# Loading Delta * u for a selective scan in two rounds of six channels, with five state buffers and loads four units ahead

## The chip, the cores and the metric

One Trainium2 chip; the kernel runs on one of its cores. The metric is the device time of one execution in microseconds (us), lower is better. Before the change three runs took 12,270.65, 12,278.37 and 12,295.46 us; their median, 12,278.37 us, is the time before. A core has five engines with a queue each: PE (matrix products), DVE (vector), ACT (activation functions), POOL (a second, slower vector engine) and SP, which here only issues DMAs; sixteen DMA engines move the data between the memory outside (DRAM) and the on-chip memory of 128 partitions.

## The reference, cut to what matters

The program is a small image network of four layers on an input of 4 x 64 x 64 x 96. Layers 0 and 1 are the costly ones. Each normalises the image, expands 96 to 192 channels, convolves 3 x 3, and runs a selective scan over the 4,096 pixels in four directions (rows, columns, and both backwards). Layers 2 and 3 are attention without softmax and a small feed-forward net. The scan, for each image, direction k, channel e and state n (16 states):

```python
# u: the convolved input, d = softplus(...): Delta, b and c: 16 numbers a step each
def step(h, inp):
    u, d, b, c = inp
    dA = jnp.exp(d[..., None] * A)
    h = dA * h + d[..., None] * b[:, :, None, :] * u[..., None]
    y = jnp.einsum('bken,bkn->bke', h, c)
    return (h, y)
```

So each step of each state needs Delta (for the decay), Delta * u (the same for all 16 states of a channel), b and c, and leaves h, which is summed over the states with c into y.

## The kernel before

The images are taken in two pairs, and each of layers 0 and 1 is run for each pair: four phases (`Scans.run`, L701). A phase has a preparation (`prepare`, L151), beside which the last phase's `finish` runs, and then a scan phase (`scan_phase`, L471). Preparation leaves in DRAM, for each chunk of 512 pixels: Delta, split in three bfloat16 parts (`ph.delta`), two copies of Delta * u (`ph.du`), and b and c (`ph.bc`). The token layers (L723 on) come last.

The 128 partitions of a scan hold 4 groups of states x 8 (direction, image) pairs x 4 states; a row of partitions is a state's number. The scan phase goes through 8 chunks of 512 pixels, and in each through 16 blocks of EB = 12 channels: 128 units, in that order. A unit is a tile h of 128 x 12 x 512 float32, which is 3 MB. Its life:

- `load` (L386): SP issues one DMA for Delta's parts (`load_delta`, L374, tile dlt, 72 partitions, L379) and six for Delta * u (`load_quarters`, L396, L401), which is replicated over the states on the way: partitions 32 to 95 take both DRAM copies, the upper quarter (96 to 127) the second copy, the lower quarter (0 to 31) the first. Each of the three is loaded in two halves of six channels. The middle two quarters are one DMA of 768 KB per half, a quarter is one of 384 KB.
- `times_b` (L408): POOL multiplies three channels at a time by b, in place, four times a unit, half a unit ahead of the scan. The first and second need the first six channels of all partitions, the third and fourth the other six.
- `replicate` (L413) and `decay` (L419): PE spreads Delta to the 128 partitions, ACT takes the exponential, channel by channel, four and three channels ahead.
- `scan` (L425): DVE runs the recurrence over 512 pixels, one instruction a channel, and overwrites Delta * u with h.
- `contract` and `evict` (L437, L454): while the next unit is scanned, PE sums h with c into y and ACT copies y out, in four parts. `store` (L462) then writes y to DRAM in four DMAs of 48 KB on SP.

The scan phase is written in a fixed order (`manual_schedule`): each engine takes its instructions in the order in which the loop (L508 to L539) names them. At the end of unit `at` SP stores unit `at - 1` (L533), loads b or c of a later chunk where one is due (L535, L537), and loads unit `at + 3` (L539). `h` has four buffers and dlt three, so unit `at + 3` takes the buffer of h that unit `at - 1` has just left. Before the loop, the prologue (L493 to L507) loads b of chunk 0, unit 0, c of chunk 0, units 1 and 2, and c of chunk 1. ACT makes the contraction's weights out of c (`weights`, L357): for chunk 0 in the prologue, for the next chunk two at a time during the units from the third on (L527).

A DMA's completion is counted on one of eight semaphores in turn, so in the program each DMA of SP in the scan phase also waits for the DMA that was issued eight before it.

Of the kernel before, what the change touches and what calls it, by code (L numbers as in the profile page):

```python
# [9 lines left out]
F32 = mybir.dt.float32  # L10
F16 = mybir.dt.float16
BF16 = mybir.dt.bfloat16
# [17 lines left out]
TC = 512  # L30
NC = L // TC
ROWS = TC // HW
EB = 12
# [4 lines left out]
DROWS = 3 * NP16 * G  # L38
DC = EB // 3
# [43 lines left out]
class Consts:  # L83
# [3 lines left out]
    def load(self, pool, name, shape):  # L87
        t = pool.tile(shape, F32, name=name)
        self.nc.sync.dma_start(t, self.a[name])
        return t  # L90
# [40 lines left out]
class Scans:  # L131
# [19 lines left out]
    def prepare(self, ph):  # L151
# [16 lines left out]
        with self.tc.tile_pool(name="prep", bufs=1) as wp, self.tc.tile_pool(  # L168
# [3 lines left out]
            def load(name, shape, at=0):  # L172
                t = wp.tile([at + shape[0]] + shape[1:], F32, name=name)
                nc.sync.dma_start(t[at:], a[pre + name])
                return t

            xp = load("x_proj", [C, 2, 2, XD2])
            dt_w = load("dt_w", [XD2 - 2 * NS, 2, E], at=2 * NS)
            conv_b = load("conv_b", [C, 2])
            ds = load("Ds", [C, 2, K])  # L180
            dsum = wp.tile([C, 2], F32, name="dsum")
# [192 lines left out]
    def load_delta(self, u):  # L374

        nc, ph = self.nc, u.ph
        u.dl = self.units.tile([DROWS, DC, TC], BF16, name="dlt", bufs=3)
        at = u.eb * EB
        nc.sync.dma_start(  # L379
            u.dl.rearrange("p e t -> p (e t)"),  # L380
            ph.delta[u.c][:, :, at : at + EB].rearrange(
                "n g (h e) t -> (n g) h (e t)", h=EB // DC
            ),
        )

    def load(self, u):  # L386

        nc, ph = self.nc, u.ph
        u.h = self.units.tile([128, EB, TC], F32, name="h", bufs=4)
        self.load_delta(u)  # L390
        n = EB // 2
        for first, quarters in ((1, 2), (3, 1), (0, 1)):
            for e in range(0, EB, n):
                self.load_quarters(u, e, n, first, quarters)

    def load_quarters(self, u, e, n, first, quarters):  # L396
# [74 lines left out]
    def scan_phase(self, ph):  # L471

        nc = self.nc
        units = [self.Unit(ph, c, eb) for c in range(NC) for eb in range(NEB)]
        last = len(units)

        def ahead(t, do):
            at, n = divmod(t, EB)  # L480
            if at < last:
                do(units[at], n)

        def b_at(t):
            at, n = divmod(t + B_LEAD, EB)
            if n % ER == 0 and 0 <= at < last:
                self.times_b(units[at], n // ER)

        with self.tc.tile_pool(name="units", bufs=2) as self.units, self.tc.tile_pool(
            name="p_a", bufs=6, space=PSUM  # L490
        ) as self.p_a, self.tc.tile_pool(name="p_y", bufs=2, space=PSUM) as self.p_y:
            with self.tc.manual_schedule():
                self.start_phase(ph)  # L493
                self.load_b(ph, 0)
                self.load(units[0])
                self.load_c(ph, 0)
                self.load(units[1])
                self.load(units[2])
                self.load_c(ph, 1)
                for t in range(-B_LEAD, 0, ER):  # L500
                    b_at(t)
                for op in range(16):
                    self.weights(ph, 0, op)
                for t in range(LEAD):
                    ahead(t, self.replicate)
                for t in range(LEAD - 1):
                    ahead(t, self.decay)  # L507
                for at, u in enumerate(units):  # L508
                    before = units[at - 1] if at else None
                    for n in range(EB):  # L510
                        t = at * EB + n
                        ahead(t + LEAD, self.replicate)
                        ahead(t + LEAD - 1, self.decay)
                        self.scan(u, n)
                        q, part = divmod(n, 3)
                        if before:
                            if part < 2:
                                self.contract(before, q, part)
                            else:
                                self.evict(before, q)  # L520
                            if n == 4 and before.c < NC - 1:
                                e = before.eb * EB
                                nc.scalar.copy(
                                    ph.carry[:, e : e + EB], before.h[:, :, TC - 1]
                                )
                        b_at(t)
                        if n == 1 and u.eb >= 2 and u.c + 1 < NC:  # L527
                            self.weights(ph, u.c + 1, u.eb - 2)
                        if n == 7 and u.eb >= NEB - 2 and u.c + 1 < NC:
                            self.weights(ph, u.c + 1, u.eb)  # L530
                        if n == EB - 1:
                            if before:
                                self.store(before)  # L533
                            if u.eb == 8 and u.c + 1 < NC:
                                self.load_b(ph, u.c + 1)  # L535
                            if u.eb == NEB - 1 and u.c + 2 < NC:
                                self.load_c(ph, u.c + 2)  # L537
                            if at + 3 < last:
                                self.load(units[at + 3])  # L539
                for q in range(4):  # L540
                    self.contract(units[-1], q, 0)
                    self.contract(units[-1], q, 1)
                    self.evict(units[-1], q)
                self.store(units[-1])
# [446 lines left out]
```

## Time and profile before

| | |
|---|---|
| median of three runs | 12,278.37 us |
| the profiled execution | 12,285.39 us, span 12,283.6 us |
| first to last scan, four phases | 1,875.7, 1,871.6, 1,874.3 and 1,874.0 us |
| busy, of the span | PE 76%, DVE 76%, ACT 58%, POOL 60% |
| SP's queue of DMAs | 2,163 MB, 52.6% of sixteen engines' time |
| h from du, in all | 1,024 DMAs of 768 KB and 2,048 of 384 KB |

The span is the time from the program's first instruction to its last in one profiled execution. Busy shares are means over stages with different limits: preparation, scan and token layers follow one another, so no engine can be judged by its share of the whole. A group's row names line, engine, operation and tiles (out<-in), the shape and count, then the busy time and the mean duration of one in ns, then the idle time of that engine just ahead of the group and what ended most of it. A wait's row names who waited for whom, the total in us, how often, and the longest. Instructions of SP only issue; the DMA goes on after them.

### The profile page before, as it was taken

To read this page: it belongs to the slowest core of one execution; us is meant where nothing else is said; L and a number is where in the kernel's file an instruction comes from. 1 tells how busy PE (TensorE), PEld (TensorE's weight loads), DVE (VectorE), ACT (ScalarE), POOL (GpSimd) and SP (SyncE) were. 2 spreads that over 40 slices of the span, in tenths; PEclk is the share of its full clock that TensorE was granted. 3 is DMA by queue.
4 is the path that set the end of the run, shared out by engine and by line. 5 is a ranking of instruction groups with operands and counts; after the bars stand their busy time and mean duration, and the time that the engine had idled before them with its cause. 6 is when DMAs were issued, how large, how long until landed. Compare 5 with 4: busy or idle time off the path is not lost.

```text
span 12283.6 us, 340681 instructions
## 1 busy us (share of the span) xinstructions
PE 9393.5 (76%) x147008; PEld 4897.8 (40%) x147008; DVE 9369.7 (76%) x9235; ACT 7066.9 (58%) x11815; POOL 7389.7 (60%) x2316
## 2 busy tenths in 40 slices
PE   7757777769877777769877777778877777777777
PEld 2224444433334444433334444443334444444333
DVE  2479999963569999982569999993459999993667
ACT  2456666643456666653456666662446666662556
POOL 0159999950149999970129999980119999990000
PEclk8669898889778988889778988888778888988787
DMA  3577777754667777764667777764567777773110
GB/s 94 170 226 256 251 252 252 251 166 140 205 206 253 251 252 255 252 201 123 183 206 253 252 251 254 251 226 125 173 194 250 253 253 252 252 252 124 19 21 11
DMA packets 906195, 2491.48 MB, mean 203 GB/s; under 512 B 278030, under 2 KB 560756, under 8 KB 773236
## 3 DMA queue, kind: packets, MB, share of 16 engines
q1 hardware_dynamic: 578036, 2163.43, 52.6%
q10 hardware_dynamic: 326656, 306.25, 8.5%
q8 instruction: 1158, 18.97, 0.7%
q14 instruction: 345, 2.83, 0.1%
HBM read 1955.47 MB, written 513.80 MB: 201 GB/s over the span
## 4 chain that ended last, share of the span: by engine, by line
DMA 57%; PE 20%; SPq 9%; DVE 5%; ACT 4%; issue 3%; POOL 1%; ACTq 1%; DVEq 0%; POOLq 0%
DMA h<-du 51%; SPq L401 8%; PE c L263 8%; PE f L596 2%; PE d L309 2%; DMA yk<-y 2%; DMA delta<-parts 1%; PE c L292 1%; PE f L687 1%; PE f L605 1%; DMA du<-du_sb 1%; POOL parts L323 1%; PE f L676 1%; DVE parts L324 1%; PE f L662 1%
## 5 line engine op out<-in xcount | busy, mean ns | idle before, releaser
L411 POOL TENSOR_TENSOR h<-h,b 128x1536 f32<-128x1536 f32 x2048 | 7019.3, 3461 | 603.8 <-DMA h<-du 230.7
L428 DVE TENSOR_TENSOR_SCAN h<-a,carry,h 128x512 f32<-128x512 f32 x5376 | 6346.6, 1259 | 238.3 <-POOL h L411 231.9
L421 ACT ACTIVATE a<-a,a_col 128x512 f32<-128x512 f32 x6144 | 4030.4, 664 | 1917.7 <-PE a L417 1885.8
L446 PEld LDWEIGHTS y<-h,cw 128*32 128x32 f32 x131072 | 2789.8, 129 | 3520.4 <-issue 1302.1
L446 PE MATMUL y<-h,cw 128*32 128x48 f32 x131072 | 3663.3, 266 | 537.8 <-DVE h L428 210.6
L417 PE MATMUL a<-dlt,rep 72*128 72x512 bf16 x6144 | 2562.4, 428 | 1339.9 <-DVE h L428 1242.8
L323 POOL CAST parts<-dl 96x1024 bf16<-96x1024 f32 x256 | 342.1, 1351 | 3108.6 <-DVE dl L320 2742.6
L319 DVE TENSOR_TENSOR du_sb<-dl,xc 96x1024 f32<-96x1024 f32 x256 | 397.0, 1577 | 1294.6 <-ACT dl L317 1242.0
L458 ACT COPY d<-y 128x384 f32<-128x384 f32 x2048 | 979.7, 478 | 490.5 <-PE y L446 449.4
L263 PE MATMUL c<-xn,taps 96*96 96x512 f32 x2304 | 1036.8, 611 | 73.7 <-DVE xn L248 52.8
L428 DVE TENSOR_TENSOR_SCAN h<-a,h 128x512 f32<-128x512 f32 x768 | 873.0, 1203 | 176.9 <-ACT a L421 139.2
L417 PEld LDWEIGHTS <-rep 72*128 72x128 bf16 x6144 | 490.8, 99 | 888.7 <-issue 646.5
L309 PE MATMUL d<-xd,dt_w 7*96 7x512 f32 x1024 | 523.0, 859 | 260.0 <-ACT xd L295 227.4
L263 PEld LDWEIGHTS c<-xn,taps 96*96 96x96 f32 x2304 | 383.6, 168 | 709.9 <-issue 631.2
L828 POOL MEMSET tn<- 1x4096 f32 x8 | 28.0, 3533 | 863.2 <-PE pa L848 514.2
L270 ACT ACTIVATE xc<-c,conv_b 96x512 f32<-96x512 f32 x128 | 87.3, 682 | 716.0 <-PE c L263 646.4
L596 PE MATMUL f<-yk,perm 128*128 128x384 f32 x1024 | 417.3, 547 | 96.6 <-DMA yk<-y 87.2
L324 DVE TENSOR_TENSOR parts<-dl,parts 96x1024 bf16<-96x1024 f32 x256 | 366.9, 1455 | 154.3 <-POOL parts L323 154.3
L317 ACT ACTIVATE dl<-d 96x1024 f32<-96x1024 f32 x256 | 252.0, 1017 | 402.3 <-DMA delta<-parts 230.6
L292 PE MATMUL c<-xc,x_proj 96*103 96x512 f32 x512 | 422.1, 961 | 2.5 <-ACT xc L270 2.5
L309 PEld LDWEIGHTS d<-xd,dt_w 7*96 7x96 f32 x1024 | 152.3, 212 | 548.3 <-ACT xd L295 299.0
L363 ACT ACTIVATE cw<-c,gmask 128x256 f32<-128x256 f32 x512 | 285.7, 569 | 119.2 <-DMA c<-bc 61.9
(114 smaller groups left out, 5656.7 us busy)
## 6 DMA issues: line engine op xcount, KB each, us to landing
h<-du SPq DMA_DIRECT2D x1024, 768.0 KB
h<-du SPq DMA_DIRECT2D x2048, 384.0 KB
delta<-parts ACTq DMA_DIRECT2D x512, 288.0 KB
dlt<-delta SPq DMA_DIRECT2D x512, 288.0 KB
du<-du_sb SPq DMA_DIRECT2D x256, 384.0 KB
du<-du_sb ACTq DMA_DIRECT2D x256, 384.0 KB
y<-d SPq DMA_DIRECT2D x2048, 48.0 KB
yk<-y SPq DMA_DIRECT2D x256, 384.0 KB
```

Of the source, the lines that this page charges most:

```text
L263: nc.tensor.matmul(rows(ps[:C]), taps[:, tap, h * C : (h + 1) * C], xn[:, ROWS * c + dy : ROWS * (c + 1) + dy, dx : dx + HW], start=tap == ...
L292: nc.tensor.matmul(rows(ps[:XD2]), xp[:, k, h], u[:, h], start=h == 0, stop=h == 1)
L309: nc.tensor.matmul(ps[:, m], dt_w[part, k, m * C : (m + 1) * C], xd[part], start=True, stop=True)
L324: nc.vector.tensor_tensor(parts[:, 2], delta, parts[:, 1], ALU.subtract)
L401: self.nc.sync.dma_start(u.h[32 * first : 32 * (first + quarters), e : e + n].rearrange("p e t -> p (e t)"), source.rearrange("a g e t -> ...
L411: self.nc.gpsimd.tensor_tensor(h, h, b, ALU.mult)
L417: self.nc.tensor.matmul(u.a[n], self.cst.rep[:, h], u.dl[:, e], start=True, stop=True)
L421: self.nc.scalar.activation(u.a[n], u.a[n], AF.Exp, scale=u.ph.a_col[:, at : at + 1])
L428: self.nc.vector.tensor_tensor_scan(u.h[:, n], u.a.pop(n), u.h[:, n], 0.0 if u.c == 0 else u.ph.carry[:, at : at + 1], ALU.mult, ALU.add,)
L446: self.nc.tensor.matmul(view(u.y[32 * j : 32 * j + 32], l2 * EB, (8 * EB, 4), (1, EB)), u.ph.cw[u.c][:, l1, 8 * j + l2], view(u.h, 64 * l1 ...
L458: self.nc.scalar.copy(u.d[:, :, :, l1], u.y[:, : 32 * EB].rearrange("p (t h x) -> p t h x", t=4, h=2))
L596: nc.tensor.matmul(ps[:, : 4 * C].rearrange("p (w v e) -> p w v e", w=4, v=nv), cst.perm[:, k], view(t, off, (sw if k < 2 else -sw, 4), (1 ...
```

## The change

The six loads of a unit come in two rounds of six channels; in a round the middle quarters come first, then the lower, then the upper quarter. There are five buffers of h and four of dlt. The prologue loads unit 3 as well, ahead of c of chunk 1, and the loop loads unit `at + 4`, into the buffer that unit `at - 1` has left. What is loaded, how large each DMA is, and all work of the other engines stay as they were.

```diff
     def load_delta(self, u):
-        u.dl = self.units.tile([DROWS, DC, TC], BF16, name="dlt", bufs=3)
+        u.dl = self.units.tile([DROWS, DC, TC], BF16, name="dlt", bufs=4)
...
     def load(self, u):
-        u.h = self.units.tile([128, EB, TC], F32, name="h", bufs=4)
+        u.h = self.units.tile([128, EB, TC], F32, name="h", bufs=5)
         self.load_delta(u)
         n = EB // 2
-        for first, quarters in ((1, 2), (3, 1), (0, 1)):
-            for e in range(0, EB, n):
+        for e in range(0, EB, n):
+            for first, quarters in ((1, 2), (0, 1), (3, 1)):
                 self.load_quarters(u, e, n, first, quarters)
...
                 self.load(units[1])
                 self.load(units[2])
+                self.load(units[3])
                 self.load_c(ph, 1)
...
-                            if at + 3 < last:
-                                self.load(units[at + 3])
+                            if at + 4 < last:
+                                self.load(units[at + 4])
```

## The prediction

> **What bounds the kernel now.** I read the page's chain first, then its groups, the waits of the SP queue, the chain of one stretch, and the busy time of short stretches. From the page, what the DMAs moved in 40 slices, and the shares of the chain by engine and by line:
>
> ```profile
> GB/s 94 170 226 256 251 252 252 251 166 140 205 206 253 251 252 255 252 201 123 183 206 253 252 251 254 251 226 125 173 194 250 253 253 252 252 252 124 19 21 11
> ...
> DMA 57%; PE 20%; SPq 9%; DVE 5%; ACT 4%; issue 3%; POOL 1%; ACTq 1%; DVEq 0%; POOLq 0%
> DMA h<-du 51%; SPq L401 8%; PE c L263 8%; PE f L596 2%; PE d L309 2%; DMA yk<-y 2%; DMA delta<-parts 1%; PE c L292 1%; PE f L687 1%; PE f L605 1%; DMA du<-du_sb 1%; POOL parts L323 1%; PE f L676 1%; DVE parts L324 1%; PE f L662 1%
> ```
>
> Half of the chain is `DMA h<-du`, the loads of Delta * u in the four scan phases (each about 1,874 us, from the first to the last scan), where the rate is flat at 250 to 256 GB/s. But POOL and DVE look nearly full too, by the groups:
>
> ```profile
> L411 POOL TENSOR_TENSOR h<-h,b 128x1536 f32<-128x1536 f32 x2048 | 7019.3, 3461 | 603.8 <-DMA h<-du 230.7
> L428 DVE TENSOR_TENSOR_SCAN h<-a,carry,h 128x512 f32<-128x512 f32 x5376 | 6346.6, 1259 | 238.3 <-POOL h L411 231.9
> ```
>
> Scans start 1.175 us apart when nothing is late (the median in the trace), so a unit of twelve needs 14.10 us of DVE; four POOL products need 4 x 3.46 = 13.84. Between 1100 and 2500 us there are 1144 scans, so a unit takes 1400 / (1144 / 12) = 14.69. DVE waits for POOL, POOL for h. Who holds h up? The SP queue's waits over the run (total us, times, longest):
>
> ```profile
> SPq L401 <- DMA h<-du: 2362.9, 1448, 3.9
> ...
> SPq L379 <- DMA h<-du: 627.0, 493, 3.6
> ...
> SPq L466 <- DMA h<-du: 344.4, 448, 3.2
> ```
>
> and the chain from 1820 to 1845 us (start, us, what):
>
> ```profile
> 1826.45 12.09 DMA h<-du
> 1838.54 0.02 issue
> 1838.56 0.69 SPq L401
> ```
>
> A load is issued 0.02 us after an earlier one has landed; SP hardly waits for a free buffer: in the program's instruction list every SP DMA waits for the DMA issued eight before it. With eleven DMAs a unit, SP is less than one unit ahead in the transfers, whatever the buffers allow. The last question is whether the DMA engines are full. Columns: stretch, busy time of five engines, clock, DMA share of 16, GB/s.
>
> ```profile
> 1844.20:1846.00 1.80, 1.80 (x50) 1.01 (x43) 1.80 (x2) 1.22 (x4) 1.80 (x1) 0.82 0.59 231
> 1835.60:1838.50 2.90, 2.73 (x67) 1.58 (x67) 2.90 (x4) 1.75 (x5) 2.85 (x2) 1.00 1.01 302
> 752.50:755.50 3.00, 0.00 (x0) 0.00 (x0) 0.00 (x0) 0.00 (x0) 0.00 (x0) 0.50 1.02 218
> 1100.00:2500.00 1400.00, 1079.69 (x25506) 609.54 (x25497) 1348.06 (x1144) 956.34 (x1705) 1302.79 (x381) 0.89 0.74 252
> ```
>
> Call the loads M (partitions 32 to 95), U (96 to 127) and L (0 to 31), each for channels 0 to 5 (0) and 6 to 11 (1); a dash marks the next unit. The completions say which is running: row one is U0 alone, 9 of 16 engines; row two L with M' beside it, all 16, 302 GB/s; row three, in the first unit of a phase, U0 with M' beside it: all 16 busy, yet only 218 GB/s. In the packet records at least eight transfers run 99% of the time from 1200 to 2100 us. So eight engines never rest, the other eight are half idle, and a unit lasts as long as those eight need.
>
> [...] M has 16 source rows and runs on all 16[...]. The trace agrees: 141 completion packets a unit, where 2 x 16 (M), 4 x 8 (quarters), 12 (dlt) and 4 x 16 (y) make 140. [...] a 12 KB packet takes 0.464 us alone, 0.92 to 0.95 with U beside M', about 0.6 with L beside M'. (That the source copy, which U shares with upper M', collides instead would have the same effect.)
>
> **The change, part by part.** *Present cost of a unit*, from mean gaps between successive completions, 1100 to 2500 us: dlt 1.04, M0 1.69, M1 1.95, U0 1.90, U1 1.88, L0 2.64, L1 2.48, four y 1.07: 14.65, as above. A half-block of four packets alone is 4 x 0.464 = 1.86; L0 and L1 together carry 1.40 more, because dlt' and M' run beside them. Everything else: 13.25.
>
> *The new order* M0 L0 U0 M1 L1 U1 has the same DMAs and bytes; what moves is who waits for what, eight back. Now: dlt' for U0, M0' for U1, M1' for L0, so M' runs beside L. After: dlt' for U0, M0' for M1, L0' for L1, U0' for U1, M1' for the first y. From the completion that frees it, a load needs 0.05 to start, 0.65 to issue (L401's median) and 0.6 to 1.15 (at 742 to 745 us) until packets flow: about 1.6. So:
> - M0' flows 1.6 us after M1 has landed. L1 takes 1.86, or about 2.35 with dlt' beside it as L0 has now (+0.5). One upper packet of M0' fits there; three meet U1 at double time: U1 + 3 x 0.464 = +1.4.
> - M1' is issued some 0.7 after U1, flows 2.3 after, beside dlt' and M0' (lower half[...]) and the start of L0': 0.545 a packet as in the 16-wide stretches without a collision, 4 x 0.08 = +0.3 on M0, +0.1 on L0. It ends 4.5 us after U1; U0' begins at 1.07 + 1.04 + 2.0 + 1.95 = 6.1.
> - Sum 13.25 + 0.5 + 1.4 + 0.3 + 0.1 = 15.55, or +0.9 a unit.
>
> The bounds: U1's collision is 2.5 to 4 packets (1.16 to 1.86), dlt's part 0.4 to 0.8, M0 and L0 0.15 to 0.7: +0.3 to +1.95 a unit. A b or c load between y and dlt (13 of 128 units) shifts the waits by one: M0' then waits for L1 and meets only U1's end, so these gain about 0.4. The first five units of a phase collide already (U0 3.84, U1 2.03 in unit 1); I take 0 there, between -10 and +10. Per phase 110 x 0.9 - 13 x 0.4 = 94 us, four phases +375.
>
> *Fifth h, fourth dlt buffer, loads four ahead.* No instruction more; each load stands one unit earlier in SP's program. With SP held by loads eight back it doesn't start earlier, so 0. Should transfers become the faster side, it would be worth part of DVE's 276 us below. *POOL may start* after the third load, not the fifth; that shifts the unit, not its period. Its second pair then waits for U1, 7.5 us after U0, against 6.9 of work.
>
> *The prologue.* Unit 3's seven DMAs pass the c load of chunk 1, which lands about 15 us later (798.95 now). ACT needs it for `weights` early in unit 2 (about 801); behind that in ACT's queue wait decays and evictions, and DVE for them. Up to 14 us a phase, but the loads of units 4 and 5 are already free to run and DVE catches up 1.4 a unit: 0 while transfers bound, +56 in all otherwise.
>
> Against the profiled execution (12,285.4 us, span 12,283.6): 12,660; the median of the runs is 7 lower: 12,653, rounded to **12,650**.
>
> **Rivals.** *Deep prefetch wins (faster).* If the collision misses U1 because M0' starts later or L1 finishes later, transfers fall below 14.1 and DVE bounds. DVE's idle time before scans is 238.3 + 176.9 (the carry-less group) less 139.2 at the four starts = 276 us: 12,002. The point that decides: upper M0' must lose less than 1.4 - 0.9 = 0.5 us to U1, one packet. For it: SP's multiple waits at M0. Against: M0' issue now follows its releasing completion within 0.1 us. *Neutral:* the eight engines carry 24 packets of h in either order, and if collisions only move, the unit stays 14.65: 12,280. Against: 218 against 302 GB/s. *Heavy:* M1' also meets U0'; the starting units, where both do, take 17.1 to 17.9; +2.5 x 440 = 13,380. Against: the 1.6 us of room before U0'.
>
> **How the numbers follow.** Forecast 0.83, faster 0.08, neutral 0.05, heavy 0.04. The forecast's bounds are +0.3 x 440 - 21 (the b and c units) = +111 and +1.95 x 440 - 21 = +837: 12,390 to 13,115. Leaving out the three rivals (0.17) and the last 0.03 at the top, where every bound would have to be at its worst, gives 12,380 to 13,000. About 0.2% is what a measurement can tell from no change: slower 0.88 (forecast, heavy and a little of neutral), same 0.04, faster 0.08.
>
> **What would show it.** Between 1100 and 2500 us some 90 units, not 95; GB/s near 238; DVE and POOL with more idle time, released by h; gaps of 3.3 us before U1's completion and about 2 before U0's; DMA share up though the rate falls. If U1 takes 1.9, the collision is wrong; if DVE's scans stand 1.175 apart throughout, prefetch was the bound.

## The result

The changed kernel takes 13,043 us (median of four runs, 13,031 to 13,052) where the kernel before takes 12,277: a ratio of 1.062, interval 1.060 to 1.064. The forecast was 12,650 with a range to 13,000: right in direction, half of the loss. The profiled span is 13,045.2 us. The four scan phases take 2,061, 2,059, 2,084 and 2,064 us against 1,874 on average, in sum 772 us more. So the loss is wholly in the scan phases, at 1.5 us a unit on average over 512 units.

The page after the change, what the DMAs moved in 40 slices and the shares of the chain:

```profile
GB/s 96 174 222 227 228 228 229 229 173 133 206 205 230 227 230 228 227 206 122 180 208 225 227 226 226 225 225 119 167 202 229 225 228 228 228 228 157 36 20 10
...
DMA 61%; PE 18%; SPq 8%; DVE 4%; ACT 4%; issue 3%; POOL 1%; ACTq 1%; DVEq 0%; POOLq 0%
DMA h<-du 55%; SPq L401 8%; PE c L263 8%; PE f L597 2%; PE d L309 2%; DMA yk<-y 1%; DMA delta<-parts 1%; PE c L292 1%; POOL parts L323 1%; PE f L606 1%; PE f L688 1%; PE f L677 1%; DVE parts L324 1%; DMA du<-du_sb 1%; DVE dl L320 1%
```

The plateau of the scan phases falls from 250 to 256 GB/s to 222 to 230, and the loads hold 55% of the chain, not 51%. The last columns of the groups are the idle time ahead of them, in us:

```profile
L411 POOL TENSOR_TENSOR h<-h,b 128x1536 f32<-128x1536 f32 x2048 | 7028.5, 3454 | 1367.2 <-DMA h<-du 621.6
L428 DVE TENSOR_TENSOR_SCAN h<-a,carry,h 128x512 f32<-128x512 f32 x5376 | 6405.8, 1261 | 889.9 <-POOL h L411 870.4
```

POOL and DVE do the same work in the same time (3.454 and 1.261 us each; an elementwise product or sum of POOL's shape, 128 x 1536 in float32, takes DVE 1.74 to 1.76 us, L650, L651 and L670) and wait 763 and 652 us longer, POOL mostly for h, DVE for POOL. PE's granted clock is lower after the change, 0.806 of full speed against 0.845, but PE holds 18% of the chain, not 20%, so this doesn't bound. SP's waits for loads (total, times, longest) grow from 3,334 to 4,220 us in the three rows:

```profile
SPq L401 <- DMA h<-du: 2639.6, 1477, 3.8
...
SPq L466 <- DMA h<-du: 811.0, 562, 3.6
...
SPq L379 <- DMA h<-du: 769.5, 496, 3.5
```

The chain from 1,500 to 1,530 us (start, us, what; L401 issues a load) has the same look as before the change, and its period can be read off it:

```profile
1512.65 0.02 issue
1512.67 0.68 SPq L401
...
1514.73 14.11 DMA h<-du
1528.84 0.02 issue
1528.86 0.68 SPq L401
```

From one release of SP to the next, 1512.65 to 1528.84, is one unit: 16.19 us. SP issues within 0.02 us of U1's completion, then sits behind the next one. Short stretches of the kernel after (columns as in the prediction):

```profile
1100.00:2500.00 1400.00, 1015.95 (x23083) 563.02 (x23082) 1232.61 (x1035) 823.07 (x1549) 1183.35 (x345) 0.84 0.74 228
1516.20:1518.80 2.60, 0.71 (x17) 0.30 (x10) 2.48 (x3) 2.60 (x7) 2.60 (x2) 1.00 0.90 249
1519.20:1522.60 3.40, 2.60 (x68) 1.51 (x67) 3.40 (x4) 2.83 (x5) 2.05 (x2) 1.00 0.55 222
```

The first row gives 1,035 scans in 1,400 us, 86 units. The other two show the eight engines that carry the quarters with company and without. Where these engines stand can be read from the semaphore counts in the trace. From 1100 to 2500 us each load M has 16 counts and each quarter nine: one 1.1 us after its issue (median) and eight from 4.0 us on, which I read as the ends on its engines. The first y store behind a unit's last quarter has 16 counts, of which eight came ahead of that quarter's first end and eight behind its ends, one by one, in all 86 units (before the change in all 95). I read this as one group of eight that carries the quarters, each engine ending its DMAs in the order of issue, and another eight that run ahead. The records don't say which half of M those other eight carry. I take it to be the upper one, because U beside them pays the double price: of the 50 packets of 12 KB that start from 752.5 to 755.5 us before the change, 43 last over 0.90 us.

After U1's completion at 1512.65, seven of the eight engines of L0 end it at 1513.15 to 1514.19 and U0 at 1517.55 to 1518.82; the last one ends M0 at 1516.15 and L0 at 1518.99. So at 1516 seven engines run U0 and only one runs L0, with the upper half of M1 beside them: 0.90 of the engines busy, 249 GB/s. At 1519 the eight with the quarters run almost alone: 0.55 busy, 222 GB/s. The other eight engines add 27 GB/s.

Here is where the time went, in mean us between successive completions, 1100 to 2500 us. A completion is the end of the last engine of a load; what the other engines did meanwhile comes further down. The last column is the fastest kernel below.

| load | before | forecast | after | e12 |
|---|---|---|---|---|
| dlt | 1.04 | 1.04 | 0.74 | 0.74 |
| M0 | 1.69 | 1.99 | 1.77 | 2.20 |
| M1 | 1.95 | 1.95 | 1.85 | 2.50 |
| L0 | 2.64 | 1.96 | **2.94** | 1.69 |
| L1 | 2.48 | 2.36 | **2.68** | 1.90 |
| U0 | 1.90 | 1.90 | 2.09 | 1.92 |
| U1 | 1.88 | 3.28 | **3.08** | 2.28 |
| y stores | 1.07 | 1.07 | 1.04 | 1.20 |
| sum | 14.65 | 15.55 | 16.19 | 14.43 |

### The profile page after: what moved, and what is told of

Read it like the earlier page. It is cut to its first block, busy times and chain, and to the rows that moved or that the text cites. A ratio compares the mean times of both kernels' runs of the same rounds, so it can differ in the third digit from the quotient of the medians.

```text
span 13045.2 us, 340148 instructions
## 1 busy us (share of the span) xinstructions
PE 9622.6 (74%) x147008; PEld 4963.4 (38%) x147008; DVE 9422.8 (72%) x9235; ACT 6818.8 (52%) x11815; POOL 7399.6 (57%) x2316
## 3 DMA queue, kind: packets, MB, share of 16 engines
q8 instruction: 1158, 18.97, 0.6%
q14 instruction: 341, 2.79, 0.1%
## 4 chain that ended last, share of the span: by engine, by line
DMA 61%; PE 18%; SPq 8%; DVE 4%; ACT 4%; issue 3%; POOL 1%; ACTq 1%; DVEq 0%; POOLq 0%
DMA h<-du 55%; SPq L401 8%; PE c L263 8%; PE f L597 2%; PE d L309 2%; DMA yk<-y 1%; DMA delta<-parts 1%; PE c L292 1%; POOL parts L323 1%; PE f L606 1%; PE f L688 1%; PE f L677 1%; DVE parts L324 1%; DMA du<-du_sb 1%; DVE dl L320 1%
## 5 line engine op out<-in xcount | busy, mean ns | idle before, releaser
L428 DVE TENSOR_TENSOR_SCAN h<-a,carry,h 128x512 f32<-128x512 f32 x5376 | 6405.8, 1261 | 889.9 <-POOL h L411 870.4
L421 ACT ACTIVATE a<-a,a_col 128x512 f32<-128x512 f32 x6144 | 3975.4, 680 | 1047.9 <-PE a L417 1029.4
L446 PEld LDWEIGHTS y<-h,cw 128*32 128x32 f32 x131072 | 2819.7, 132 | 3904.9 <-issue 2557.3
L417 PE MATMUL a<-dlt,rep 72*128 72x512 bf16 x6144 | 2753.0, 453 | 1822.5 <-DVE h L428 1743.1
L458 ACT COPY d<-y 128x384 f32<-128x384 f32 x2048 | 1024.5, 500 | 2209.9 <-DMA y<-d 1551.5
L417 PEld LDWEIGHTS <-rep 72*128 72x128 bf16 x6144 | 528.1, 100 | 1206.9 <-issue 904.1
```

The lines of the kernel that those rows point to most:

```text
L417: self.nc.tensor.matmul(u.a[n], self.cst.rep[:, h], u.dl[:, e], start=True, stop=True)
L421: self.nc.scalar.activation(u.a[n], u.a[n], AF.Exp, scale=u.ph.a_col[:, at : at + 1])
L428: self.nc.vector.tensor_tensor_scan(u.h[:, n], u.a.pop(n), u.h[:, n], 0.0 if u.c == 0 else u.ph.carry[:, at : at + 1], ALU.mult, ALU.add,)
L446: self.nc.tensor.matmul(view(u.y[32 * j : 32 * j + 32], l2 * EB, (8 * EB, 4), (1, EB)), u.ph.cw[u.c][:, l1, 8 * j + l2], view(u.h, 64 * l1 ...
L458: self.nc.scalar.copy(u.d[:, :, :, l1], u.y[:, : 32 * EB].rearrange("p (t h x) -> p t h x", t=4, h=2))
```

## The experiments

Times are medians of four runs (twenty for e2b, buffers and lead alone, and for the first of the three with twelve DMAs); each ratio is to the kernel before on the same chip, with its interval. M, U, L, 0, 1 and the dash are the names of the prediction; "gaps" are those of the table above.

### Which part of the change

**Order alone.** The new order in the kernel before, with four buffers and three units ahead.

```diff
-        for first, quarters in ((1, 2), (3, 1), (0, 1)):
-            for e in range(0, EB, n):
+        for e in range(0, EB, n):
+            for first, quarters in ((1, 2), (0, 1), (3, 1)):
```

> The kernel before with the new order of the six loads alone (M0 L0 U0 M1 L1 U1), four buffers of h, three of dlt, loads three units ahead. If the order is the whole cause: as after, 13,040 us within 40, a unit 16.0 to 16.1 us. If the fifth buffer, the unit more of lead or the later load of c is the cause: 12,280 within 60. A time between divides the loss between the two.

13,053 us, 1.0617 (1.0590 to 1.0643): the order is the whole loss.

**Buffers and lead alone.** Five h, four dlt, loads four units ahead, the old order.

> Five buffers of h, four of dlt and loads four units ahead, with the order of the loads as before. If the order is the whole cause and SP is held by the load eight back: 12,280 within 40, a unit 14.65. If lead and buffers are worth something where transfers are not slowed: down to 12,100. If they are the cause of the loss: about 13,040.

12,303 us, 1.0013 (1.0006 to 1.0020). With SP held by the load eight back, a fifth buffer brings nothing that can be measured. The small loss fits the prediction's late c load at a phase's start: there the slowest unit of a phase, the third, takes 24.5 to 25.8 us, where it took 13.4.

### Which neighbour is slow

**Source copies exchanged** (the changed kernel; the upper quarter reads copy 0, the lower copy 1).

```diff
-        copies = slice(0, 2) if quarters == 2 else slice(first % 2, first % 2 + 1)
+        copies = slice(0, 2) if quarters == 2 else slice(1 - first % 2, 2 - first % 2)
```

> The kernel after with the source copies of the two quarters exchanged: U (partitions 96 to 127) reads copy 0, L (0 to 31) copy 1; the upper half of M still reads copy 1. Two theories of why U1 beside the next M0 is slow. Write side (the partitions of U and of upper M): nothing changes, 13,040 within 40, the gap before U1's completion stays near 3.1 us and that before L0's near 2.9. Source side (both read copy 1): U1's gap falls to about 2.4 and L0's and L1's rise, to 3.7 and 3.2, since they then share the copy; the time may change little, the gaps tell.

13,057 us, 1.0622 (1.0606 to 1.0637). U1 3.01, L0 2.71, L1 2.81: the time doesn't follow the copy.

**Lower quarter first** (the kernel before, whose M' runs beside the last two quarters; these are now U0 and U1).

```diff
-        for first, quarters in ((1, 2), (3, 1), (0, 1)):
+        for first, quarters in ((1, 2), (0, 1), (3, 1)):
```

> The kernel before with the two quarters exchanged in the order, all else as before: M0 M1 L0 L1 U0 U1, so that the next unit's M, which waits for L1 and U0 now, runs beside U where it ran beside L. If U and the upper half of M collide by their partitions: U0 and U1 carry six to eight packets at double time in place of L's 1.4 us, a unit 16.0 to 17.0, 12,950 to 13,400. If any load of eight engines slows alike beside M: 12,280 within 40.

12,233 us, 0.9951 (0.9936 to 0.9967): a little faster. The forecast's premise, that a completion beside M' costs double for U and little for L, falls here. U0 and U1 take 2.32 and 3.16, together 5.48, where L0 and L1 took 5.12; the rest of the unit gives more back. One stretch in the first unit of a phase looks like L1 (partitions 0 to 31) beside the upper half of M' (64 to 95), since L1 completes at 758.21:

```profile
756.50:758.20 1.70, 0.00 (x0) 0.00 (x0) 0.00 (x0) 0.00 (x0) 0.00 (x0) 0.50 0.98 202
```

It shows another pair. Six of the eight engines ended L1 by 756.70 and U0 at 759.86 to 760.56, so most of them were in U0, in the same half of the partitions as the upper half of M'. The 202 GB/s agree with the 218 of the prediction's third row.

**Rounds with the upper quarter first** (the changed kernel, order M0 U0 L0 M1 U1 L1).

> The kernel after with U ahead of L in each round: M0 U0 L0 M1 U1 L1. M0 of the next unit flows 1.6 us after M1, so it meets the end of U1 and then L1; M1 of the next unit now runs beside U0 where it ran beside L0. If U collides by its partitions: U0's gap 3.7 to 4.0, L0's about 2.1, U1's and L1's 2.7 each, a unit 16.5, 13,280 within 120. If U and L are slowed alike: the gaps follow the place in the order (2.9, 2.1, 2.7, 3.1), 13,040 within 60. If loads beside L cost nothing, as forecast: 12,650.

12,515 us, 1.0190 (1.0173 to 1.0207). The first quarter behind M0 completes late whichever it is: U0 3.19 here, L0 2.94 in the changed kernel. Only the last two differ: U1 2.22 and L1 2.37, in sum 4.59, against 5.76. So which quarter comes last matters, but not as the forecast's rule had it.

**dlt behind the h loads** (the changed kernel).

```diff
-        self.load_delta(u)
         n = EB // 2
         for e in range(0, EB, n):
             for first, quarters in ((1, 2), (0, 1), (3, 1)):
                 self.load_quarters(u, e, n, first, quarters)
+        self.load_delta(u)
```

> The changed kernel with the unit's dlt load issued after its six h loads instead of before them; M0' still waits for the same load (M1) and L0' for L1. If the next unit's dlt' beside L1 is what makes L1 slow (2.68 us between completions against 1.87 bare), L1 falls to 2.2 or less, the unit by 0.3 to 0.5 us, and the time to 12,790 to 12,890. If it is M0' that costs there, or the total of bytes in flight, L1 stays within 0.2 of 2.68 or the cost turns up beside dlt's new place, and the time stays at 12,990 to 13,100.

12,938 us, 1.0533 (1.0518 to 1.0549). L1 falls to 2.31, but dlt takes 1.27 and U0 2.63: a part of the cost of L1 was dlt', and most of it turned up at dlt's new place.

**Another row pitch in DRAM** (the changed kernel).

```diff
-PITCH = 2
+PITCH = 5
```

> The changed kernel with the rows of Delta * u in DRAM padded by 5 channels in place of 2, so that the addresses of the eight groups and of the two copies stand differently to each other; nothing else moves. If packets that take 0.7 to 0.9 us do so because the addresses read at one time collide in DRAM, L0, L1 and U1 (2.94, 2.68 and 3.08 us) move by more than 0.2 us and the time leaves 12,990 to 13,090. If it is only how many engines move data at once and in which order, the time is 13,043 within 0.2%.

13,046 us, 1.0621 (1.0604 to 1.0637); L1 2.71, U1 3.06, L0 2.75. The addresses that rows and copies have to each other play no visible part.

### When M' runs

**Thirteen DMAs a unit** (the changed kernel, two of the four y stores in two parts each). With the wait for the DMA eight back, two more DMAs hold M0' until U1 has landed.

> The kernel after with two of the four y stores of a unit split in two (the same packets), so thirteen DMAs a unit in place of eleven and a wait for the DMA eight back that is later in the unit: M0 of the next unit waits for U1, not M1, and can't run beside L1 and U1. If the loss is made by the next unit's M running beside the quarters: U1's gap falls to about 2.1, L1's to 2.3, a unit to 14.6, 12,400 within 120. If it is made by the order in itself (say by half the channels at a time) whatever runs beside: 13,040 or a little more, for two more issues a unit.

13,203 us, 1.0742 (1.0726 to 1.0758). L1 and U1 fall to 1.89 and 1.93, the time of a quarter alone: what made their completions late is that M0' and dlt' were let in beside them. But M0 rises to 3.47, since it now starts too late, and U0 to 2.93, with M1' beside it.

**Twelve DMAs**, in the kernel before, in the changed one, and in the kernel before with the lower quarter first.

```diff
-            self.nc.sync.dma_start(
-                u.ph.y[row : row + 4, :, b, :, u.eb].rearrange("j g h x -> (j g) h x"),
-                u.d[t::4, t].rearrange("p h l x -> p h (l x)"),
-            )
+            for h in (slice(0, 1), slice(1, 2)) if t < 1 else (slice(0, 2),):
+                self.nc.sync.dma_start(
+                    u.ph.y[row : row + 4, :, b, h, u.eb].rearrange("j g h x -> (j g) h x"),
+                    u.d[t::4, t, h].rearrange("p h l x -> p h (l x)"),
+                )
```

> The kernel before with one of the four y stores of a unit split in two (the same packets): twelve DMAs a unit, so the next unit's M0 waits for L0 and M1 for L1, one DMA later than before, and both run mostly beside y, dlt and the lower half of M. If the upper half of M costs only beside a quarter: L1's gap falls from 2.5 to about 2.1, 12,100 within 80. If sixteen engines at work cost the same beside anything: 12,280 within 50.

> The kernel after with one y store split in two: twelve DMAs a unit. The next unit's M0 waits for L1, not M1, and reaches only U1's end; M1 still runs beside L0 and perhaps U0. If M0 beside U1 is what makes U1 slow: U1's gap falls from 3.1 to 2.1 to 2.4, L0 stays near 2.9, a unit 15.7, 12,870 within 100. If not: 13,040 or more. In the run with thirteen the engines also ran short of loads (M0 3.47); with twelve there should be no such gap.

> The kernel before with the lower quarter ahead of the upper (0.995 by itself) and one of the four y stores in two parts, so that a unit has 12 DMAs and the next M0' waits one load later (0.998 by itself). If the two add up, 0.992 to 0.995 and 12,190 to 12,220. The rival: the later wait takes from M0' the start that the quarters beside it paid for already, and the two gains are the same gain: 0.995 to 0.998.

Before with twelve: 12,270 us, 0.9984 (0.9978 to 0.9991). Changed with twelve: 12,660 us, 1.0302 (1.0287 to 1.0317), so half of the loss goes by one small DMA more: L1 1.90, U1 2.20, while L0 and U0, near which M1' still flows, take 2.61 and 2.86. Lower first with twelve: **12,057 us, 0.9819 (0.9796 to 0.9842)**, faster than both kernels and more than the two gains by themselves would add up to.

Why the last one is fast can be read from where M' stands. It has both M loads first and holds M0' until U0 has landed, M1' until U1 has. The first of their engines end 2.4 and 4.6 us after U1, the eighth 2.9 and 5.3 us after it, beside dlt', M0' and M1' themselves (lower halves), and no quarter but the end of U1 has company:

```profile
1518.30:1520.20 1.90, 1.90 (x62) 1.27 (x53) 1.90 (x3) 0.73 (x2) 1.90 (x1) 0.83 0.97 317
1523.20:1530.50 7.30, 5.79 (x137) 3.21 (x136) 7.30 (x7) 5.47 (x10) 6.18 (x3) 1.00 0.69 232
```

In the first stretch M loads have the engines to themselves, mostly M1's lower half beside its own upper half (14 of 16 engines ended M0 by 1519.09, M1 at 1520.31 to 1522.08): 317 GB/s at 0.97 busy. Set it against 249 GB/s at 0.90 for mostly U0 beside M1's upper half in the changed kernel. The packets have the same 12 KB, and the pairing decides. With that DVE bounds the unit (its groups):

```profile
L411 POOL TENSOR_TENSOR h<-h,b 128x1536 f32<-128x1536 f32 x2048 | 7023.1, 3465 | 377.2 <-DMA h<-du 190.9
L428 DVE TENSOR_TENSOR_SCAN h<-a,carry,h 128x512 f32<-128x512 f32 x5376 | 6330.8, 1261 | 66.5 <-POOL h L411 65.5
```

DVE's idle time ahead of scans is 66.5 us, where it was 238.3 before and 889.9 after the change; the median unit takes 14.10 us, twelve scans at 1.175.

### What the partitions do

**Two loads of 64 partitions a round**, 0 to 63 and 64 to 127 (the kernel before; four h loads a unit, all on 16 engines).

```diff
-        for first, quarters in ((1, 2), (3, 1), (0, 1)):
+        for first, quarters in ((0, 2), (2, 2)):
```

> The kernel before, its buffers and lead, with each round loaded as two loads of 64 partitions (0 to 63, then 64 to 127, both rounds in turn) in place of one of 64 and two of 32: four loads of 768 KB a unit, each on all 16 engines[...]. If the loss and the bound come from lower engines that carry more packets than the upper ones, at the 0.6 to 0.74 us a packet measured with all engines at work the unit needs 16 x 0.6 to 0.74 plus 1.8 for dlt and y, 11.4 to 13.6 us, below VectorE's 14.1: a unit falls from 14.65 to about 14.2 to 14.4, 512 units save 130 to 230 us, and the time is 12,050 to 12,150. If every load on all 16 engines runs at the 0.93 us a packet that some stretches show, it is 16.7 us a unit and 13,300.

13,827 us, 1.1267 (1.1244 to 1.1290). In the order before, the eight engines with the quarters carry 24 packets of 12 KB a unit (eight of M, sixteen of the quarters) and the other eight carry eight; these are the lower and the upper engines of the expectation. Here each carries 16. The loads take 3.2 to 3.9 us each, a packet of 12 KB 0.94 us in the median (half of them 0.90 to 0.96). From 1100 to 2500 us the rate is 207 GB/s with 97% of the engines busy, and the page's slices are flat:

```profile
GB/s 96 185 207 206 207 207 209 208 173 123 200 196 208 209 207 208 207 204 118 171 202 207 210 208 207 207 209 115 175 196 209 204 210 211 209 207 161 56 19 9
```

The sources are those of M. At the start of a phase in the kernel before, M0 and M1 run alone on all 16 engines, at 410 GB/s:

```profile
748.00:749.50 1.50, 1.50 (x5) 0.59 (x4) 0.00 (x0) 0.00 (x0) 0.00 (x0) 0.50 1.00 410
```

Only the partitions written differ: M puts one half of its packets below partition 64 and one above.

**M moved to 0 to 63 or 64 to 127**, with the other two quarters behind it: in the order before, in the rounds (the edit below), in the rounds mirrored, and in the order before with twelve DMAs.

```diff
-            for first, quarters in ((1, 2), (0, 1), (3, 1)):
+            for first, quarters in ((0, 2), (2, 1), (3, 1)):
```

> The kernel before with the load of 64 partitions moved from 32 to 95 down to 0 to 63[...] and the two single quarters 64 to 95 and 96 to 127 behind it. Theory of the halves: partitions 0 to 63 share about 210 GB/s among all engines that write them, and 64 to 127 another 210. Then the next unit's upper halves, which run beside the single quarters, no longer meet them: the two quarters beside them fall from 2.64 and 2.48 us to 1.9 each, while the part of M1' that runs beside M0' meets it now and costs up to 1 us: 12,000 to 12,280. Rival: a packet of 12 KB beside a single quarter takes 0.6 to 0.74 us whichever partitions they write: the quarters stay at 2.4 to 2.7 us and the time at 12,230 to 12,400.

> The changed kernel with the same move: each round loads 0 to 63, then 64 to 95, then 96 to 127. Theory of the halves: M1' beside the first quarter and M0' beside the last two no longer share anything with them, the three slow slots (2.94, 2.68 and 3.08 us) fall to about 1.9, 3 us of the unit's 16.1 go, and VectorE's 14.1 us a unit is the bound: 12,000 to 12,250. Rival, that any upper half beside any quarter costs 0.6 to 0.74 us a packet: 12,950 to 13,150.

> The mirror: each round loads 64 to 127 on all 16 engines, then 0 to 31, then 32 to 63. Theory of the halves: as the run above, 12,000 to 12,250. If one pair of quarters behaves unlike the other, this run and the one above differ. Rival: 12,950 to 13,150.

> The kernel before with 0 to 63 as the load of 64 partitions and one y store in two parts (12 DMAs a unit), so that the next unit's upper halves run beside M0' and M1' lower halves and not beside the quarters. Theory of the halves: both lie in partitions 0 to 63 now, so M0' and M1' take over 3 us each in place of 2.0 and 2.9 with the same 12 DMAs, and the time is 12,400 to 13,000. Rival, that an upper half beside a lower half of such a load is cheap wherever it is put: 12,250 to 12,300.

13,534 us (1.1013, 1.0997 to 1.1029), 12,855 us (1.0464, 1.0424 to 1.0505), 13,176 us (1.0738, 1.0712 to 1.0765) and 13,556 us (1.1033, 1.1016 to 1.1049). The last is plainest. In the twelve-DMA order, M' halves run beside each other: with M at 32 to 95 that was the cheap pairing, with M at 0 to 63 it is the dearest. M0 takes 3.67 us, where it takes 1.98 in the kernel before with twelve DMAs, and 46 of the 47 packets of 12 KB that start in this stretch last 0.9 to 1.0 us:

```profile
1521.00:1523.80 2.80, 2.40 (x58) 1.32 (x61) 2.80 (x4) 1.49 (x4) 2.80 (x2) 0.52 1.01 206
```

So two quarters in one half of the partitions share about 210 GB/s: 206 in this stretch and 207 with two halves. Why they do is not shown.

But e13 to e15, the first three of these, didn't come out as that rule alone says. Quarters and the upper half of M lie in different halves there, and the first quarter behind M0 still took 2.39 and 2.54 us in the rounds (e14) and their mirror (e15), the last 3.28 and 3.10, where 1.9 was expected. In part the runs spoiled their own test: M's two halves now collide with each other, and the loads of the next M reach the last quarter. In part the completions hide what happened, since they are those of one late engine. The same gaps, for the median of a quarter's eight engines (mean us, 1100 to 2500 us; by place in the order, the completions' gap behind the stroke):

| quarter | before | after | e14 |
|---|---|---|---|
| first of round 0 (L0) | 1.88 / 2.64 | 1.93 / 2.94 | 1.66 / 2.39 |
| second of round 0 (U0) | 1.84 / 1.90 | **3.74** / 2.09 | **2.08** / 2.04 |
| first of round 1 (L1) | 2.21 / 2.48 | 1.87 / 2.68 | 1.83 / 2.44 |
| second of round 1 (U1) | 1.86 / 1.88 | 2.12 / 3.08 | 1.99 / 3.28 |

On most engines the rule holds. In the changed kernel U0 is the quarter that flows beside the upper half of the next M1, in the same half of the partitions, and takes 3.74 us (in part waiting for its issue); in e14, where that half of M lies elsewhere, it takes 2.08, and in e15 2.24. The slow completions of L0, L1 and U1 in the changed kernel and in e14 are almost wholly those of the last engine.

**Common source copy taken away** in e14 and e15 (both single quarters read copy 0, the upper half of M copy 1).

```diff
-        copies = slice(0, 2) if quarters == 2 else slice(first % 2, first % 2 + 1)
+        copies = slice(0, quarters)
```

> The rounds with 0 to 63 as the load of 64 partitions, and both single quarters (64 to 95 and 96 to 127) reading copy 0 of Delta * u, where 96 to 127 read copy 1 before; the upper half (32 to 63) reads copy 1 as ever. If a quarter that reads the same copy as the upper half beside it is slowed by that, whatever partitions they write, the last quarter of a unit falls from 3.28 us to 2.4 or less, the unit by 0.8 and the time from 12,855 to 12,400 to 12,550. If the source plays no part, it stays at 12,855 within 0.6%.

> The mirror: 64 to 127 as the load of 64 partitions, both single quarters (0 to 31 and 32 to 63) reading copy 0, the upper half (96 to 127) copy 1. If the common copy is what slows the last quarter (3.10 us), it falls to 2.4 or less and the time from 13,176 to 12,700 to 12,900; if not, 13,176 within 0.6%.

12,866 us (1.0472, 1.0457 to 1.0488) and 13,161 us (1.0712, 1.0689 to 1.0734); the last quarters stay at 3.31 and 3.14. The copy is out.

Put together, this is the share of the time from 1100 to 2500 us in which more than 13 of the 16 engines move data, and the rate then, from the packet records:

| kernel | share | GB/s then | unit's sum or result |
|---|---|---|---|
| before | 37% | 309 | 14.65 us |
| after | 39% | 274 | 16.19 us |
| e12 | 33% | 330 | 14.43 us |
| e16, M in one half, M beside M | 47% | 213 | 1.103 |
| e9, all loads in one half each | 90% | 215 | 1.127 |

## Why the prediction was wrong in size

**Right.** The bound is the loads' transfers and SP's wait for the DMA eight back. The order is the cause (e1b), the fifth buffer, fourth dlt and lead are worth about nothing (e2b), and the late c load costs little: 5.5 to 8.0 us in the first five units of a phase. M0' flows while L1 and U1 are not yet complete, and with M0' held back they are fast (e4b). That U1 took 3.08 where 3.28 was forecast is partly luck: the forecast slowed all its engines, and the median engine takes 2.12. M1' is issued 0.83 us after U1's completion (forecast 0.7). POOL and DVE wait for h. Between 1100 and 2500 us there are 86 units at 228 GB/s, where 90 and 238 were forecast.

**The step that failed: M1' and the room ahead of U0'.** The forecast had the upper half of M1' flow at 0.545 us a packet, beside dlt' and M0', end 4.5 us after U1, 1.6 us ahead of U0', and so cost L0' 0.1. The first engine of M1' ends 6.6 us after U1 and the eighth 7.2, and the room did not exist. The forecast added up completions as if all engines of a load moved together, which put the start of U0' at 6.1. U0' is issued when U1 completes, and seven of its engines are through with L0' by then or soon after: their U0' packets start 1.5 us after U1's completion (1514.11 to 1514.20 in the unit above), and the upper half of M1' joins them from 1515.35 on. From 1516.2 to 1517.2 the 18 packets of 12 KB that start last 0.79 to 0.94 us, 13 of them over 0.90, the price that the prediction gives for two loads in one half. The last engine is in L0' at that time, and L0 took 2.94 where 1.96 was forecast. That is +0.98 us, against the 0.64 by which the unit was underestimated. L1 (+0.32) and U0 (+0.19) add to it; dlt, M0, M1, U1 and the y stores (-0.85 together) give back.

**The premise behind it.** I took the load that completes next for the load that runs. The row at 1835.6 with 302 GB/s stood for L beside M'; but six of the eight engines had ended L1 by 1835.66 and ended M0' at 1838.30 to 1838.83, so it shows mostly M0', its lower half beside its upper half. So the prediction had no price for L beside M'. The rule of the halves is real (e9, e16, U0 in e14), and the changed order meets it: M1' flows beside U0'. In the order before, the first engine of M1' ended 2.43 us after L1 and the eighth 2.97, mostly beside dlt' and M0', which the fast kernel shows to be the cheap place. The new order took that place away, and this is the part that the forecast priced at 0.4 us.

**The neutral rival** said that the same 24 packets on eight engines give the same time in either order. It falls with the unit's 16.19 us: the packet's price depends on its neighbour. **The faster rival** fell with U1 at 3.08. **The heavy one** (M1' meets U0' too) named what happened on seven of eight engines, and the argument against it, the 1.6 us of room, was the error. Its size, +2.5 us a unit, was too large: +1.5 was measured.

**Smaller points.** I expected the loss in 110 units of a phase and none in the first five. It is 193 us a phase; the first five lose 5.5 to 8.0 us, nearly all in the third unit, behind the late c load, and the rest about 1.5 us each. The units ahead of a b or c load gain more than the 0.4 forecast: U1 takes 2.32 and 2.24 us in these two of a chunk's sixteen, 3.1 in the rest.

**What stays open.** Why one of eight engines stays behind in most orders with eleven DMAs, and why its completions of L0, L1 and U1 take 2.7 to 3.1 us while the others need about 1.9 to 2.1. It isn't the source copy (e3b, e17, e18) or the row pitch (e11); dlt' explains a part of L1 (e10). It isn't the pages of the program's own instructions either, which the DMA engines fetch as well (8 or 16 KB, two or three a unit; 1,158 packets with 18.97 MB and 341 with 2.79 MB in the two queues of the kind "instruction" of the changed kernel's page): in the changed kernel L0, L1 and U1 take 2.94, 2.65 and 3.07 us where none is in flight for more than 0.1 us of them. From unit to unit the gap of L0 hardly repeats between the four phases (correlations of 0.02 to 0.33), so a fixed pattern of addresses is unlikely. That the order causes the loss is shown; how much of the 1.5 us is the collision of M1' with U0', and how much the late engine's own, is not.

## What to carry to other kernels

In this kernel, where loads of different width share the DMA engines, the order of issue decides which loads run beside each other, and with the same bytes that moved it by 6% one way (e1b, the order alone) and 2% the other (e12, with one store in two parts). Before costing a load that runs ahead, find the price of a packet for each pair of neighbours from the trace, in steady running, and ask in which slot the run-ahead part ends. Ask it of most engines and of the last one separately: a load's completion is only its last engine's. A cheap way to shift it is the number of DMAs between a load and the one it waits for: one more small store did here what a fifth 3 MB buffer could not.

## What the runs showed of the hardware that I had not expected

One engine sets the pace. The prediction said that eight engines never rest, since eight transfers always run. The completion counts say otherwise: a quarter's load ends on eight engines, and in the changed kernel seven of them finish U1 at 1523.40 to 1524.09 us, the eighth at 1528.84. On average the last engine of a load is 1.5 to 2.8 us behind the next to last, 1.0 to 1.7 in the kernel before, and 0.4 to 0.8 in e12. SP waits for the last one, while the other engines are already at the next M0', and in that time packets of 0.8 to 1.2 us stand in the records. It doesn't look like an engine that is slow by itself: with twelve or thirteen DMAs a unit (e4b, e6, e7, e12, e16) the last engine is 0.1 to 0.9 us behind. There the next M0' waits for a load one or two later. That an engine, once late, has its last quarters still to do when M0' comes, and so stays late, would fit this, and is not shown. The records don't name the engine.

The halving is abrupt: a 12 KB packet takes 0.46 to 0.47 us on eight engines or on all sixteen with M alone (410 GB/s), and mostly 0.9 to 1.0 us with two quarters of one half (e9, e16). A fast neighbour exists too, M's lower beside M's upper half in steady running, at 317 GB/s (e12).
